# The last block's queries and values by seven half-size products: one more block in a chain, its sums kept in the keys of the block before

## The chip, the cores and the metric

The kernel runs on one core of a Trainium2 chip. Five engines work side by side, each in the order of its own instruction list: TensorE (PE in the profile) multiplies matrices, VectorE (DVE), ScalarE (ACT) and GpSimd (POOL) work on tiles, and SyncE (SP) issues transfers. ACT and POOL issue transfers too. Semaphores order the engines among each other: an instruction waits until a count is reached, and everything behind it on its engine waits with it. The time is the device time of one execution in microseconds (us). The median of three runs stands for the kernel.

## The reference

Two layers work on the same layer-normed input, and a gated sum leaves the kernel:

```python
xn = layernorm(x)                                   # 2 x 2048 rows of 512
q, k, v = norm2(xn) @ qkv                           # a second norm with gamma, beta
s = softmax(causal(q @ k.T / sqrt(512))) @ v @ o_proj + xn
scores = xn @ gate_w.T + gate_b + bias              # 8 experts, the best 2 of each row
y[e] = silu(xn @ w1[e].T + b1[e]) @ w2[e].T + b2[e]  # 512 -> 352 -> 512
g = silu(sum of the 2 chosen experts' y, weighted by a softmax of their scores)
out = x + s * g
```

All of it is in float32.

## The kernel before, in words

The 4096 rows are 32 tiles of 128 rows, in eight blocks of four tiles (`NB = 8`, `TB = 512` rows). The kernel folds the weights first: `wqk` (queries' weight times keys' weight) and `wvo` (values' weight times output weight), each 512 x 512. Then three stages follow, and TensorE runs through all of them.

**Stage 1, projections.** For each block b, `kT` holds the normed rows turned (called keys, 128 partitions x 4 x 512). Two results are made of it: queries `wqk x kT`, stored in `qt_d[b]`, and values `kT x wvo`, stored in `v_d[b]`. An *item* is a pair (block, queries or values): item 0 is the queries of block 0, item 1 its values, and so on. For blocks 0 to 6 (`items`, 14 of them) a 512-cube product is cut into quarters and done by seven half-size products in place of eight, by Winograd's form: four sums of quarters of the weight (`weight_sums`, made once) and four sums of quarters of the keys (`key_sums`, made per block by POOL) stand as factors, and the products are added up in four PSUM banks a to d. `one_product(i, k)` does product k (1 to 7) of item i: four matmuls of 256 columns, then copies by ACT from the bank into the output tile. Product 5 goes to a bank of its own, is copied out as `p5`, and is added to two quarters of the output by DVE (`with_fifth`, L395 in the profile). `chain_of_products()` gives the order: the products of item i end while those of item i + 1 begin. When a queue of stores (`unstored`) is emptied, in product 3, the finished item before is sent to DRAM; from block 5 on by ACT's queue.

Block 7 is done otherwise: `unit(7, u)`, u = 0 to 7, makes a quarter of its queries (0 to 3) or values (4 to 7) by four matmuls of 512 columns, copies the bank into a tile `j` and stores it from ACT's queue. Two of these units stand inside the end of the chain (`None` in `chain_of_products`), six behind it.

**Where the tiles lie.** The memory called `arena` is that of the experts' second weights `w2`, which are loaded late. Until then its six equal areas hold the weight sums of the queries (area 0) and of the values (area 1), the key sums (areas 2 to 4, by `2 + b % 3`) and one output (5). Expert e of `w2` takes three quarters of an area: experts 0 to 2 lie over areas 0, 1 and half of 2. The outputs of items 10, 12 and 13 are in two tiles of the keys' pool `kp` (`late_outs`, `so` in the profile). When stage 1 ends (`stage_a.close()`), the memory of `kp`, of `wqk`/`wvo` and of the staging tiles is given to two later tiles among others: `keep`, a mask that POOL writes (L1414), and `w1s`, sums of the experts' first weights that DVE writes (L1108). Their first writes wait for the last reader of what lay there.

**Stage 2, routing and experts.** `route()` is a generator that turns the gate scores into lists of rows per expert, on DVE mostly. It stands between the last units of stage 1: each `yield n` lets n steps of the projections pass. It ends in `toki` (which rows go into which slot), from which POOL gathers rows, and in the tables `eidi`, `b1sel`, `share`. DVE builds one-hot matrices in eight groups (`at`, `mine`, `which`), and TensorE adds each up with eight small matmuls (`inv_p`, L744). The experts' steps follow. In step i POOL gathers the rows of slot i + 6 (`xs`), SP's queue turns slot i + 4 (`turn`, L1041, `xhT`), DVE joins the halves of slot i + 1 into `xT` (`join`, L1046), PE makes `ph` of slot i (`up`, L1086), ACT scales it into `h`, POOL splits it into `hu` (L1166), SP's queue turns `hu` (L1170), DVE joins it into `ht` (L1175) for slot i - 2, ACT applies silu, and PE makes `py` of slot i - 3 (`down`, L1195). So steps 0 to 2 have no `down`, and step 3 has the first. The expert of a slot is known only at run time, so `down` reads all of `w2`. The first weights' sums `w1s` are made in steps 0 to 6, by DVE but for one.

**Stage 3** is the attention, with the rest.

The order of every engine's instructions is the program's own (`manual_schedule`); no planner moves them. Loads of `w2` come from SP's queue: three transfers for each expert (512 KB, 192 KB, and 2 KB of `b2`). SP's and ACT's transfers signal on eight semaphores taken in turn, and each transfer waits, on the engine that issues it, for the one that last used its semaphore.

Of the kernel before, what the change touches and what calls it, by code (L numbers as in the profile page):

```python
# [26 lines left out]
def gated_attention_moe(  # L27
# [411 lines left out]
    def unit(b, u):  # L439

        kT = kts[b]
        po = banks[(u + 3) % ND]
        r = u % ND
        for c in range(ND):
            if u < ND:
                nc.tensor.matmul(
                    po, lhsT=wqk[:, c, ts(r, P)], rhs=kT[:, c, :],
                    start=(c == 0), stop=(c == ND - 1),
                )
            else:  # L450
                nc.tensor.matmul(
                    po, lhsT=kT[:, c, ts(r, P)], rhs=wvo[:, c, :],
                    start=(c == 0), stop=(c == ND - 1),
                )
        o = stg.tile([P, TB], F32, name=f"j_{b}_{u}", tag="stg")
        nc.scalar.copy(o, po)
        nc.scalar.dma_start(out=(qt_d if u < ND else v_d)[b][:, r, :], in_=o)

# [19 lines left out]
    def key_sums(b):  # L478

        assert all(k != b for _, _, _, k in pending)  # L480
        s = ksums[b] = four(2 + b % 3)
        b11, b12, b21, b22 = (
            kts[b][:, 2 * i : 2 * i + 2, ts(j, HD)] for i in range(2) for j in range(2)
        )
        nc.gpsimd.tensor_tensor(s[:, 0], b12, b11, ALU.subtract)
        nc.gpsimd.tensor_tensor(s[:, 1], b22, s[:, 0], ALU.subtract)
        nc.gpsimd.tensor_tensor(s[:, 2], b22, b12, ALU.subtract)
        nc.gpsimd.tensor_tensor(s[:, 3], b21, s[:, 1], ALU.subtract)
# [4 lines left out]
    items = [(b, of_q) for b in range(SEVEN) for of_q in (True, False)]  # L493
    FIFTH = {}

    def chain_of_products():
        yield from ((0, k) for k in (1, 5, 2, 6))
        for i in range(len(items) - 1):
            for j, k in (1, 1), (0, 3), (0, 7), (1, 5), (0, 4), (1, 2), (1, 6):
                yield i + j, k  # L500
        for k in (None, 3, 7, None, 4):
            yield len(items) - 1, k

    def one_product(i, k):
# [4 lines left out]
        b11, b12, b21, b22 = (  # L509
            kts[b][:, 2 * i : 2 * i + 2, ts(j, HD)] for i in range(2) for j in range(2)  # L510
        )
        if k == 2 and i in (first_late, first_late + 2):
# [4 lines left out]
            else late_outs[int(i == first_late + 2)] if k in (2, 3, 7, 4) else raw[:, : ND * D]  # L517
# [28 lines left out]
        elif k == 5:  # L546
            multiply(bank_d, s[:, 0], t[:, 0], start=True)
            FIFTH[i] = stg.tile([P, TB], F32, name=f"p5_{i}", tag="stg")
            nc.scalar.copy(FIFTH[i], bank_d)
        elif k == 2:  # L550
            multiply(bank_a, a12, b21)
            nc.scalar.copy(place(0, 0), whole(bank_a))
        elif k == 6:
            multiply(bank_b, s[:, 1], t[:, 1])
# [8 lines left out]
        elif k == 7:  # L563
            multiply(bank_c, s[:, 2], t[:, 2])
            with_fifth(place(1, 1), bank_c)
            del FIFTH[i]
        else:
            multiply(bank_c, a22, t[:, 3])
            nc.scalar.copy(place(1, 0), whole(bank_c))
# [9 lines left out]
    def route():  # L579

        with ExitStack() as rt:
# [210 lines left out]
            for i in range(FIRST):  # L792
                gather(i)

# [21 lines left out]
            nc.vector.tensor_copy(eidi, eid)  # L816
            nc.vector.tensor_scalar(eid, eid, -1.0, float(E), ALU.mult, ALU.add)
# [91 lines left out]

    def pieces():  # L910

        n = 0
        for i, k in chain_of_products():
            if k is None:
                unit(*units.pop(next(j for j, (b, _) in enumerate(units) if b == SEVEN)))
                yield
                continue
# [8 lines left out]
        while units:  # L926
            add_due(0)
            unit(*units.pop(0))
            while unstored:
# [1011 lines left out]
```

## Time and profile before

| | us |
|---|---|
| median of three runs | 1008.28 (1007.41 to 1008.75) |
| the profiled execution | 1007.83 |
| its span (first to last instruction) | 1006.0 |
| PE busy in the span | 999.9 |
| start of item 13's product 1 on PE | 198.51 |
| start of the first unit of block 7 | 212.23 |
| start of the first `up` | 246.92 |
| start of the first `down` | 256.39 |
| start of `keep` on POOL | 247.15 |

The profile says when each instruction began and how long it took. In a row of the timeline the first number is the start, the second the time, then engine, line and tiles; "x8" counts records, and a float32 matmul leaves two. Brackets give the idle time of that engine just before the row, and what ended it. ACTq and SPq are the issuing parts of ACT and SP. "KB each, us to landing" is the median time from a transfer's issue to its completion, where the trace has it. TensorE's granted clock is 1.0 through the whole span.

### The profile page before, as it was taken

The numbers are of one execution on the slowest core, as the hardware profiler recorded it, in microseconds if no ns is written. First come the engines' busy times: TensorE is split into PE (matmuls) and PEld (weight loads), VectorE is DVE, ScalarE is ACT, GpSimd is POOL, SyncE is SP. The second block draws the span as 40 slices with busy tenths as digits, with TensorE's granted clock in tenths as the row PEclk, the third lists the DMA queues.
The fourth block names the chain that finished last, engine by engine and source line by source line (L and its number), as shares of the span: only waits on it lengthen the run. The fifth ranks groups of instructions, "written<-read, shape, count | busy, mean of one in ns | idle before, by whom it ended". The sixth has DMA issues, their size and how long they took to land. (4 is left out here: it accounts for less than half of the span.)

```text
span 1006.0 us, 13431 instructions
## 1 busy us (share of the span) xinstructions
PE 999.9 (99%) x3924; PEld 665.3 (66%) x3924; DVE 716.9 (71%) x1396; ACT 403.2 (40%) x804; POOL 483.3 (48%) x475
## 2 busy tenths in 40 slices
PE   9999999999999999999999999999999999999998
PEld 5888888874567767766753448677675544447577
DVE  6996746897887777677744579668576556878667
ACT  3344445322444454444445112232335535442241
POOL 4474564004644454444332165254557776764272
PEclk9999999999999999999999999999999999999999
DMA  8689996978999999999999576274677768753361
GB/s 293 193 264 293 329 286 258 349 249 240 202 227 220 211 208 221 217 200 222 216 218 242 164 193 147 78 206 104 183 199 239 225 200 240 207 141 86 92 165 42
DMA packets 296647, 207.96 MB, mean 207 GB/s; under 512 B 230776, under 2 KB 243832, under 8 KB 296576
## 3 DMA queue, kind: packets, MB, share of 16 engines
q1 hardware_dynamic: 282432, 163.56, 63.2%
q0 software_dynamic: 10400, 34.63, 12.5%
q10 hardware_dynamic: 3744, 8.91, 2.4%
q8 instruction: 34, 0.56, 0.2%
q14 instruction: 37, 0.30, 0.1%
HBM read 92.35 MB, written 60.03 MB: 151 GB/s over the span
## 5 line engine op out<-in xcount | busy, mean ns | idle before, releaser
L1195 PE MATMUL py<-arena,ht 128*128 (+3 forms) x396 | 176.7, 593 | 0.0
L1307 PE MATMUL ps<-k,q 128*128 128x512 f32 (+3 forms) x416 | 143.0, 495 | 0.3 <-PEq L1455 0.3
L1495 POOL COPY pu<-pT 128x1024 uint16<-128x1024 uint16 (+2 forms) x74 | 82.5, 1146 | 118.1 <-ACT pT L1485 59.1
L1166 POOL COPY hu<-h 128x704 uint16<-128x704 uint16 x66 | 61.9, 956 | 155.8 <-issue 121.7
L1195 PEld LDWEIGHTS py<-arena,ht 128*128 128x128 f32 (+3 forms) x396 | 71.8, 185 | 80.7 <-issue 76.9
L1307 PEld LDWEIGHTS ps<-k,q 128*128 128x128 f32 x416 | 74.7, 190 | 67.1 <-issue 56.5
L970 POOL DMA_INDIRECT xs<-zu_d,toki x66 | 77.6, 1176 | 70.2 <-DVE toki L791 55.6
L1181 ACT ACTIVATE ht<-ht,b1sel 128x128 f32<-128x128 f32 (+3 forms) x216 | 67.9, 380 | 88.1 <-DVE ht L1175 88.1
L1145 DVE TENSOR_TENSOR h<-p,h 128x176 f32<-128x176 f32 x182 | 55.5, 337 | 60.7 <-PE p L1138 57.2
L1678 POOL DMA_INDIRECT yg<-y_d,posi x64 | 67.4, 1053 | 36.9 <-DVE yg L1689 21.9
L1535 PE MATMUL po<-v,pT 128*128 128x512 f32 x152 | 67.9, 592 | 0.0
L347 POOL COPY zu<-z 128x1024 uint16<-128x1024 uint16 x32 | 39.9, 1245 | 55.7 <-DVE z L332 55.7
L1517 DVE COPY pT<-puT 128x1024 uint16<-128x1024 uint16 (+2 forms) x74 | 54.1, 759 | 8.8 <-DMA puT<-pu 8.6
L1485 ACT ACTIVATE pT<-pT,nm 128x1024 f32<-128x1024 f32 x14 | 16.1, 1148 | 110.3 <-DVE nm L1395 72.0
L1203 ACT COPY y<-py 128x512 f32<-128x512 f32 x55 | 32.2, 585 | 62.3 <-PE py L1195 48.4
L1485 ACT ACTIVATE pT<-ps,nm 128x512 f32<-128x512 f32 (+3 forms) x52 | 30.1, 581 | 62.5 <-DVE nm L1395 38.8
L1365 DVE TENSOR_TENSOR pT<-p,pT 128x512 f32<-128x512 f32 x49 | 32.9, 687 | 25.8 <-PE p L1359 22.1
L1535 PEld LDWEIGHTS po<-v,pT 128*128 128x128 f32 x152 | 28.6, 190 | 31.9 <-issue 30.1
L1707 POOL TENSOR_TENSOR o<-o,yg 128x512 f32<-128x512 f32 x30 | 42.0, 1398 | 14.3 <-DVE o L1699 14.1
L1699 DVE SCALAR_TENSOR_TENSOR o<-xo,xscale,o 128x512 f32<-128x512 f32 x30 | 25.9, 871 | 30.1 <-ACT o L1696 30.1
L1046 DVE COPY xT<-xhT 128x1024 uint16<-128x1024 uint16 x66 | 45.2, 712 | 2.3 <-DMA xhT<-xs 2.0
L1708 POOL TENSOR_TENSOR o<-o,xo 128x512 f32<-128x512 f32 x30 | 43.0, 1432 | 2.4
(342 smaller groups left out, 2142.9 us busy)
## 6 DMA issues: line engine op xcount, KB each, us to landing
y_d<-y SPq DMA_DIRECT2D x66, 256.0 KB, 4.4
zu_d<-zu SPq DMA_DIRECT2D x32, 264.0 KB, 2.8
kt_d<-kT SPq DMA_DIRECT2D x16, 512.0 KB, 5.9
q<-qt_d SPq DMA_DIRECT2D x32, 256.0 KB, 5.4
k<-kt_d SPq DMA_DIRECT2D x32, 256.0 KB, 4.7
v<-v_d SPq DMA_DIRECT2D x32, 256.0 KB, 5.6
xo<-in_x_dram SPq DMA_DIRECT2D x32, 256.0 KB, 3.8
x<-in_x_dram SPq DMA_DIRECT2D x30, 256.0 KB, 4.9
```

What stands on the lines that cost most here:

```text
L970: nc.gpsimd.indirect_dma_start(out=xs, out_offset=None, in_=zu_d, in_offset=bass.IndirectOffsetOnAxis(ap=toki[:, order[i] : order[i] + 1], ...
L1046: nc.vector.tensor_copy(xT.bitcast(U16).rearrange("p c (t h) -> p c t h", h=2), xhs.pop(i).rearrange("p (h c) t -> p c t h", h=2),)
L1145: nc.vector.tensor_tensor(out, x, y, ALU.add)
L1166: nc.gpsimd.tensor_copy(hu[:, :, :H], h.bitcast(U16).rearrange("p (d h) -> p h d", h=2))
L1181: nc.scalar.activation(ht[:hn, c, at], ht[:hn, c, at], AF.Silu, bias=b1sel[:hn, c, j : j + 1])
L1195: nc.tensor.matmul(py[at, :], lhsT=ht[:k, c, at], rhs=rhs[n], start=(c == 0), stop=(c == NH - 1),)
L1307: nc.tensor.matmul(ps[:, :w], lhsT=aqs[seq[s] // 2][:, c, ts(t % 2, P)], rhs=aks[first + j][:, c, :w], start=(c == 0), stop=(c == ND - 1),)
L1485: nc.scalar.activation(turned[s][:, at:end], src, AF.Exp, bias=nm, accum_out=rs[:, j : j + 1])
L1495: nc.gpsimd.tensor_copy(pu[:, : 2 * w].rearrange("p (h d) -> p h d", h=2), turned[s][:, k : k + w].bitcast(U16).rearrange("p (d h) -> p h ...
L1517: nc.vector.tensor_copy(turned[s][:, k : k + w].bitcast(U16).rearrange("p (i t h) -> p i t h", t=P, h=2), puT[:, : 2 * w // P, :].rearrang ...
L1535: nc.tensor.matmul(dst, lhsT=turned[s][:, ts(k, P)], rhs=avs[first + k // BT][:, k % BT, cols], start=(start and k == k0), stop=(k == k1 - 1),
L1678: nc.gpsimd.indirect_dma_start(out=y, out_offset=None, in_=y_d, in_offset=bass.IndirectOffsetOnAxis(ap=posi[k][:, n : n + 1], axis=0),)
```

## The change

Items 14 and 15 (block 7's queries and values) join the chain, so stage 1 has 16 items of seven products. `unit` is gone. What goes with it:

- `key_sums(7)` writes its four sums over the quarters of the keys of block 6, one or two at a time, behind products 1, 2 and 3 of item 13, which are the last to read those quarters. POOL does it, ahead of its first gathers.
- The outputs of items 14 and 15 go to the two `late_outs`, those of items 12 and 13 before. The stores go out from ACT's queue, those of item 15 behind the last product.
- In the last step products 6 and 2 change places, and product 2 of item 15 empties the queue of stores.
- `w2` of expert 3 is loaded fifth; experts 0, 1 and 2, which lie over the weight sums, are loaded behind the last product in SP's order, behind the first four turns of `xs` and ahead of the fifth.
- `route()` has two more `yield 1`.
- In steps 0 to 4 `join` is done two slots ahead; DVE thus does slots 0 to 2 ahead of its first `w1s`.

```diff
-    def unit(b, u):
-        kT = kts[b]
-        po = banks[(u + 3) % ND]
...
     def key_sums(b, parts=range(4)):
-        s = ksums[b] = four(2 + b % 3)
+        s = ksums[b] = (
+            [four(2 + b % 3)[:, k] for k in range(4)] if b < SEVEN
+            else [quarter_keys(b - 1)[k] for k in (1, 0, 2, 3)]
+        )
+        b11, b12, b21, b22 = quarter_keys(b)
+        of = (b12, b11), (b22, s[0]), (b22, b12), (b21, s[1])
+        for k in parts:
+            nc.gpsimd.tensor_tensor(s[k], *of[k], ALU.subtract)
-    items = [(b, of_q) for b in range(SEVEN) for of_q in (True, False)]
+    items = [(b, of_q) for b in range(NB) for of_q in (True, False)]
     def chain_of_products():
         yield from ((0, k) for k in (1, 5, 2, 6))
         for i in range(len(items) - 1):
-            for j, k in (1, 1), (0, 3), (0, 7), (1, 5), (0, 4), (1, 2), (1, 6):
+            last = i == len(items) - 2
+            for j, k in (1, 1), (0, 3), (0, 7), (1, 5), (0, 4), *(((1, 6), (1, 2)) if last else ((1, 2), (1, 6))):
                 yield i + j, k
-        for k in (None, 3, 7, None, 4):
+        for k in 7, 3, 4:
             yield len(items) - 1, k
...
-            else late_outs[int(i == first_late + 2)] if k in (2, 3, 7, 4) else raw[:, : ND * D]
+            else late_outs[int(i in (first_late + 2, first_late + 4))] if k in (2, 3, 7, 4) else raw[:, : ND * D]
...
         elif k == 2:
             multiply(bank_a, a12, b21)
             nc.scalar.copy(place(0, 0), whole(bank_a))
+            while unstored and i == len(items) - 1:
+                store(*unstored.pop(0))
...
             for i in range(FIRST):
                 gather(i)
+            yield 1
...
             nc.vector.tensor_copy(eidi, eid)
+            yield 1
...
+    SUMS_BEHIND = {1: (0, 1), 2: (2,), 3: (3,)}
...
             one_product(i, k)
+            if i == 2 * SEVEN - 1 and k in SUMS_BEHIND:
+                key_sums(SEVEN, SUMS_BEHIND[k])
             scale_next()
             n += 1
             if n * 4 // 7 > (n - 1) * 4 // 7:
                 units.pop(0)
+                if not units:
+                    add_due(0)
+                    while unstored:
+                        store(*unstored.pop(0))
                 yield
...
-    w2_left = [4, 5, 6, 7, 0, 1, 2, 3]
+    w2_left, w2_last = [4, 5, 6, 7, 3], [0, 1, 2]
...
-            if done >= W2_FROM:
+            if done >= W2_FROM and w2_left:
                 load_w2(w2_left.pop(0))
...
-        if i + 1 not in xts:
-            at(join, 1)
+        for k in (1, 2) if 0 <= i < 5 else (1,):
+            if i + k not in xts:
+                at(join, k)
...
             next(projected)
-            if w2_left:
-                load_w2(w2_left.pop(0))
-    while w2_left:
-        load_w2(w2_left.pop(0))
+    for e in w2_left + w2_last:
+        load_w2(e)
     stage_a.close()
```

More of the change, by code (lines that the diff above doesn't have):

```diff
@@ L437, in keep_scores @@
         )
-    def unit(b, u):
-        kT = kts[b]
-        po = banks[(u + 3) % ND]
[L443 to L457, printed above, removed]
     SEVEN = NB - 1
@@ L476, in weight_sums, with quarter_keys, key_sums @@
         lhs_sums(wsums[name], w)
[L478 removed]
+    def quarter_keys(b):
+        return [kts[b][:, 2 * i : 2 * i + 2, ts(j, HD)] for i in range(2) for j in range(2)]
+    def key_sums(b, parts=range(4)):
         assert all(k != b for _, _, _, k in pending)
[L481 to L493 removed]
+        s = ksums[b] = (
+            [four(2 + b % 3)[:, k] for k in range(4)] if b < SEVEN
+            else [quarter_keys(b - 1)[k] for k in (1, 0, 2, 3)]
+        )
+        b11, b12, b21, b22 = quarter_keys(b)
[3 more added lines that the diff above has]
+    items = [(b, of_q) for b in range(NB) for of_q in (True, False)]
     FIFTH = {}
@@ L508, in one_product @@
         a11, a12, a21, a22 = (w[:, 2 * j : 2 * j + 2, ts(i, HD)] for i in range(2) for j in range(2))
-        b11, b12, b21, b22 = (
-            kts[b][:, 2 * i : 2 * i + 2, ts(j, HD)] for i in range(2) for j in range(2)
-        )
+        b11, b12, b21, b22 = quarter_keys(b)
         if k == 2 and i in (first_late, first_late + 2):
@@ L546, in one_product @@
         elif k == 5:
-            multiply(bank_d, s[:, 0], t[:, 0], start=True)
+            multiply(bank_d, s[:, 0], t[0], start=True)
             FIFTH[i] = stg.tile([P, TB], F32, name=f"p5_{i}", tag="stg")
@@ L552, in one_product @@
             nc.scalar.copy(place(0, 0), whole(bank_a))
+            while unstored and i == len(items) - 1:
+                store(*unstored.pop(0))
         elif k == 6:
-            multiply(bank_b, s[:, 1], t[:, 1])
+            multiply(bank_b, s[:, 1], t[1])
             nc.scalar.copy(bank_c, bank_b)
@@ L563, in one_product @@
         elif k == 7:
-            multiply(bank_c, s[:, 2], t[:, 2])
+            multiply(bank_c, s[:, 2], t[2])
             with_fifth(place(1, 1), bank_c)
+        else:
+            multiply(bank_c, a22, t[3])
+            nc.scalar.copy(place(1, 0), whole(bank_c))
             del FIFTH[i]
-        else:
-            multiply(bank_c, a22, t[:, 3])
-            nc.scalar.copy(place(1, 0), whole(bank_c))
             queue = nc.sync if b < LATE else nc.scalar
@@ L913, in pieces @@
         for i, k in chain_of_products():
[L914 to L917, printed above, removed]
             made[0] = n
@@ L924, in pieces @@
                 units.pop(0)
+                if not units:
+                    add_due(0)
+                    while unstored:
+                        store(*unstored.pop(0))
                 yield
[L926 to L929, printed above, removed]
-                store(*unstored.pop(0))
-            yield
     def sum_keys(i):
```

## The prediction

> **What bounds the kernel now.** I read the page's shares first, then the waits of PE, then the timeline of each engine from 185 to 275 us, where stage 1 ends. The chain that ended last goes back only to 568 us and does not reach the change.
>
> ```profile
> PE 999.9 (99%) x3924; PEld 665.3 (66%) x3924; DVE 716.9 (71%) x1396; ACT 403.2 (40%) x804; POOL 483.3 (48%) x475
> ...
> PE warm L870 <- DVE b1s L181: 1.1, 1, 1.1
> ```
>
> PE is busy 999.9 of 1006.0 us and its longest wait anywhere is 1.1 us, at the start. So PE work that goes away is time, one for one, unless PE has to wait instead; and there is no idle time of PE to pay with. PE's timeline around the change:
>
> ```profile
> 210.50 1.89 PE L526 MATMUL bank_b<-arena 128*128 128x256 f32 x8
> ...
> 223.60 1.11 PE L744 MATMUL inv_p<-which,at 128*128 128x136 bf16 x16
> ...
> 226.32 3.60 PE L446 MATMUL bank_b<-kT,wqk 128*128 128x512 f32 x8
> 229.76 3.60 PE L446 MATMUL bank_c<-kT,wqk 128*128 128x512 f32 x8
> ...
> 246.92 9.63 PE L1086 MATMUL ph<-w,xT 128*128 x32
> 256.39 2.74 PE L1195 MATMUL py<-arena,ht 128*128 x6
> ```
>
> From start to start a unit takes 3.435 us (226.32 to 229.76) and a half-size product 1.727 (210.50 to 212.23, the first unit). The four `up` fill 246.92 to 256.4, and the first `down` follows with no gap. What it waited for is in the rows of DVE, ACT, POOL and SP's queue, in this order:
>
> ```profile
> 222.85 0.72 DVE L777 TENSOR_TENSOR which<-mine,tile 128x544 bf16<-128x544 bf16 x1
> ...
> 247.12 0.89 DVE L1108 TENSOR_TENSOR w1s<-w 128x704 f32<-128x704 f32 x1 [6.23 <-PE bank_c L451]
> ...
> 254.96 0.59 DVE L1175 COPY ht<-huT 128x768 uint16<-128x768 uint16 x1 [2.64 <-DMA huT<-hu]
> ...
> 230.95 9.05 ACTq L575 DMA_DIRECT2D v_d<-so  x2
> ...
> 240.05 0.59 ACT L456 COPY j<-bank_c 128x512 f32<-128x512 f32 x1 [9.51 <-DVE so L395]
> ...
> 247.15 0.20 POOL L1414 MEMSET keep<- 128x128 f32 x1 [6.00 <-PE bank_c L451]
> ...
> 250.16 0.81 POOL L1166 COPY hu<-h 128x704 uint16<-128x704 uint16 x1 [0.38 <-ACT h L1164]
> ...
> 229.93 11.76 SPq L1041 DMA_TRANSPOSE xhT<-xs  x5
> ```
>
> Three things are to be seen. `keep` on POOL and the first `w1s` on DVE stood idle 6 us and began when PE ended its last unit, whose memory they take. From `keep` a chain leads to the first `down`: `keep`, a gather, `hu` at 250.16, its turn from 251.00 landing for `ht` at 254.96, silu from 255.59, `down` at 256.39. That chain had at most 0.4 us to spare. And a store that waits stops ACT: the two `v_d<-so` held ACT's queue 9 us, and the copy of a bank behind them came 9.5 us late (PE wrote that bank again only at 243.49, so it cost nothing).
>
> **The change, part by part.**
>
> *PE work.* Eight units go, 8 x 3.435 = 27.5 us; fourteen products come, 14 x 1.727 = 24.2. Sum: -3.3 us.
>
> *Key sums of block 7.* Four POOL operations of 1.27 to 1.49 us (the rows of the earlier key sums). POOL is idle from 170 to 225.8 us, and nine products or more (15 us) lie between product 1 of item 13 and the first use. Nothing; without that cover up to 5.5 us.
>
> *ACT copies.* Eight of 0.59 us go and fourteen come; ACT is busy 5.0 of 22 us there. Nothing in themselves.
>
> *DVE's adds and the index groups.* Item 13's two adds (1.29 us) now stand ahead of the last group, which ended at 223.57 in the trace (222.85 + 0.72). Group seven ends at 219.75, so the adds run to 220.97 and the last group takes 3.2 more: 224.15. PE's order there, from 212.23: products 14/1 and 13/3, eight index matmuls (0.47), 13/7, 0.47, 14/5, 13/4, 0.47: it is at the last group at 222.27. **PE waits 1.9 us.** `toki`, and with it the gathers from 225.8 and the turns from 229.9, stay where they were within 0.2 us; PE's last twelve products follow from 224.67 on, 1.727 each.
>
> *Stores on ACT.* The two `v_d` stores of item 13 stand ahead of the copy that frees bank c for product 14/4; the second waits for the semaphore of the first turn (`xhT`, 229.93; turns land after 3.9 to 7.6 us, median 5.8). With 5.1 it is 235.0, the copy ends 236.05, and 14/4, due at 235.03, begins at 236.2: **1.1 us** (0 to 2.5).
>
> *Second weights behind.* The program's waits say more than the diff here. Expert 0's first transfer (512 KB) stands in SP's queue behind the fourth turn, so it is issued at about 240.0 (the fourth turn ended at 239.65 in the trace, the fifth began at 240.28). The store of item 14's queries on ACT waits for the same semaphore, so for that load to land; behind the store stand the copies of item 15, one of which frees bank c for the last product, 15/4. How long does the load take? Two bounds:
>
> ```profile
> qt_d<-so ACTq DMA_DIRECT2D x4, 512.0 KB, 6.3
> ...
> v_d<-so ACTq DMA_DIRECT2D x2, 512.0 KB, 3.1
> v_d<-j ACTq DMA_DIRECT2D x4, 256.0 KB, 4.7
> ```
>
> From below 3.1, from above 8.4 (the slowest `so` store). The Trainium skill, "DMA: Bandwidth & Descriptors", section "Anatomy of one DMA", gives 2.0 us and the bytes at 436 GB/s, here 3.2 us (fitted on GpSimd's path). I take 6.0: the load is on the queue of two turns still under way, and a turn in this stretch took up to 7.6; the DMA engines are busy 0.93 from 225 to 247. So it lands at 246.0, the two stores are issued by 246.7, the copy of bank c ends at 247.35, and 15/4, due at 244.85, runs from 247.5 to 249.2: **2.6 us**. By the rule it would land at 243.2 and cost nothing here.
>
> *The last stores.* Item 15's two stores follow the copy of 15/4: issued 249.95 to 250.65. They read `late_outs`, which lie in the memory of `keep` and `w1s`, and both now wait for these stores to land, where they waited for PE before. While they fly, so do item 14's stores and expert 2's load. If stores of ACT's queue ran beside SP's loads undisturbed, 3.1 would do. The same page, section "Issuing engines are not separate DMA queues", speaks against this change: transfers issued from different engines run on the same 16 engines and interleave. With that, 4.7: between the median of all `so` stores (4.3) and the 6.3. So `keep` begins at **255.0**, not 247.15; with 3.1 at 253.4.
>
> *Where it goes next.* Queued behind `keep` on POOL are the seventh gather and `hu` of slot 0; behind `w1s` on DVE the join of slot 3. `hu` follows `keep` after 2.8 us, takes 0.8, its turn lands 3.0 to 4.0 later, join and first silu take 1.0: `down` 8.4 us behind `keep` (9.2 in the trace, with what it had to spare, and the quicker turns that follow, 2.8 us). So `down` begins at 263.4 against 256.39: **+7.0 us**. Slot 3's join is done at 255.0 + 1.8 + 0.7 = 257.5; its `up`, due at 256.3, waits 1.2 of that. The early joins help slots 1 and 2 alone, which were never late. From `down` on the order is the old one, and PE full: the shift stays to the end.
>
> *Sum.* -3.3 + 1.9 + 1.1 + 2.6 + 4.7 (PE free at 258.7, `down` at 263.4) = +7.0. The profiled execution would be 1007.83 + 7.0 = 1014.8 (span 1013.0), the median 1008.28 + 7.0 = **1015.3**. By the two rules' short durations alone (3.2 for load and stores) `keep` begins at 251.3, `down` at 259.7: +3.3, 1011.6.
>
> **Rivals.**
>
> *The saving comes through (faster).* It is PE's pace that sets the end. Place: `keep`'s wait. For -2.0 us `down` must begin by 254.4, so `keep` by 246.0. For it: POOL and DVE were idle there, and the DMA engines' row of this stretch falls to one tenth at 246. Against it: with the index wait the last product ends at 245.4 at the earliest, its copy and two issues take 1.3, the quickest such store 2.6: 249.3. Without any wait it would be -3.3, 1005.0; with the index wait alone -1.4, no longer faster by what can be told.
>
> *The waits on PE are real, the gate has cover.* If `hu` and its turn had more to spare than I read, what is left is -3.3 + 1.9 + 1.1 + 2.6 = +2.3: 1010.6. For it: the four `up` give PE 9.5 us of work after the last product. Against: the gate falls 6 us behind the last product, and the chain from it takes 8.4.
>
> *Crowded DMA.* The load lands at 248 and the stores take 6.5: `keep` at 259, `down` at 267.4, +11: 1019.3. For it: both durations were seen within this stretch. Beyond, more than 1020.
>
> *Quick DMA.* Load by 243 and stores in 3: `keep` at 251, or near 249.5 with no wait on PE but the index one: +1.5 to +3, the upper part slower, the lower no change.
>
> **How the numbers follow.** A measurement of this kernel tells apart what differs by 0.2%, 2.0 us. The likeliest case, the gate of the last stores with its load between 3.2 and 8 us, spans 1011.6 to 1019.3 and has 0.68; crowded beyond 1019.3: 0.10; the gate covered: 0.10; quick DMA with no change: 0.08; the saving through: 0.04. So slower 0.88, same 0.08, faster 0.04. The range 1010.3 to 1020.0 leaves out the two last cases and the far end of crowding.
>
> **What would show it.** Products of items 14 and 15 at 1.73 us each; 1.5 to 2 us of PE's idle ahead of the last eight index matmuls, put down to DVE `which`; ACT held at the `qt_d<-so` stores until after 243; `keep` and `w1s` waiting for a transfer of `v_d`, and starting after 250; a gap of PE ahead of the first `down`. I am wrong if `keep` begins before 249, if the first load lands within 3 us, or if `down` follows `up` with no gap although `keep` is late.

## The result and the profile after

The changed kernel takes 1026.49 us (median of 6 runs, 1024.28 to 1028.56), the kernel before 1008.41 (6 runs beside it): 1.0183 times as long, 95% interval 1.0169 to 1.0197, that is +18.1 us where +7.0 was predicted. The profiled execution has a span of 1024.4 us against 1006.0. One run of e10 below, 1043.41 us, was in a slower state of the chip; its figures are of the other three.

The page's shares and, under the dots, the waits of PE in the changed kernel (line waited for, us in total, times, longest):

```profile
PE 1000.9 (98%) x3972; PEld 676.0 (66%) x3972; DVE 724.7 (71%) x1400; ACT 405.9 (40%) x810; POOL 486.8 (48%) x479
...
PE ph L1067 <- DVE xT L1027: 6.8, 1, 6.8
PE inv_p L725 <- DVE which L758: 4.4, 3, 2.9
PE bank_c L505 <- ACT so L518: 2.8, 2, 1.5
PE py L1176 <- ACT ht L1162: 1.8, 1, 1.8
...
PE p L1119 <- issue: 1.1, 1, 1.1
```

Where PE's longest wait had been 1.1 us, at the start, there are now five kinds of wait, 16.9 us together, all between 200 and 295 us. PE's timeline there (start, us, engine, line, operation, idle time before it and its end):

```profile
213.16 1.89 PE L505 MATMUL bank_a<-kT,wqk 128*128 128x256 f32 x8
214.89 1.89 PE L505 MATMUL bank_b<-arena,kT 128*128 128x256 f32 x8
...
227.37 0.63 PE L725 MATMUL inv_p<-which,at 128*128 128x136 bf16 x8 [2.92 <-DVE which L758]
...
250.08 2.00 PE L505 MATMUL bank_c<-wvo,kT 128*128 128x256 f32 x8 [1.27 <-ACT so L518]
251.93 7.34 PE L1067 MATMUL ph<-w,xT 128*128 x24
266.07 4.88 PE L1067 MATMUL ph<-w,xT 128*128 x8 [6.80 <-DVE xT L1027]
272.75 2.85 PE L1176 MATMUL py<-arena,ht 128*128 x6 [1.80 <-ACT ht L1162]
```

The products stand 1.73 us apart, as costed. The first `up` starts at 251.93 (246.92 before), the first `down` at 272.75 (256.39): +16.4 us. The fourth `up` took 4.88 us where the three ahead of it took 7.34 together. The rows of the other engines behind these waits:

```profile
200.83 2.29 DVE L747 TENSOR_TENSOR at<-lane,part 128x1024 bf16<-128x1024 bf16 x1
...
212.48 1.80 DVE L752 TENSOR_TENSOR mine<-slot_b,part 128x544 bf16<-128x544 bf16 x1
...
217.47 1.67 DVE L758 TENSOR_TENSOR which<-mine,row 128x544 bf16<-128x544 bf16 x1
...
248.50 0.82 ACTq L556 DMA_DIRECT2D qt_d<-so  x2
...
252.73 1.07 ACTq L556 DMA_DIRECT2D v_d<-so  x2
...
263.61 0.20 POOL L1394 MEMSET keep<- 128x128 f32 x1 [20.09 <-DMA v_d<-so]
...
263.60 0.89 DVE L1089 TENSOR_TENSOR w1s<-w 128x704 f32<-128x704 f32 x1 [11.04 <-DMA v_d<-so]
```

Three rows of DVE are each about 1 us longer than their like (`at` is 1.22 elsewhere, `mine` and `which` 0.72). The last two stores are issued from 252.73 on, and `keep` and `w1s` wait for them until 263.6.

The third view is one that the prediction did not use: busy time of the engines in long stretches, of before and then of after (from:to, length, PE, PEld, DVE, ACT, POOL, granted clock, mean share of the DMA engines, GB/s).

```profile
212.00:232.00 20.00, 20.00 (x88) 12.13 (x87) 18.29 (x32) 5.60 (x9) 4.95 (x5) 1.00 0.75 248
232.00:248.00 16.00, 16.00 (x40) 7.31 (x39) 9.47 (x15) 2.93 (x5) 4.44 (x12) 1.00 0.99 289
```

```profile
212.00:232.00 20.00, 16.27 (x99) 14.08 (x98) 18.97 (x25) 4.68 (x9) 5.90 (x4) 1.00 0.28 96
232.00:248.00 16.00, 14.48 (x68) 12.47 (x66) 11.56 (x23) 5.64 (x10) 5.12 (x13) 1.00 0.98 263
248.00:264.00 16.00, 10.00 (x36) 6.31 (x34) 2.90 (x5) 4.05 (x6) 0.32 (x2) 0.99 0.91 244
```

From 212 to 232 us the kernel before moves 20 x 0.248 = 5.0 MB, the changed one 1.9 MB. By queue (packets, MB, share of the engines; q1 is SP's queue, q10 ACT's), before and then after:

```profile
q1 hardware_dynamic: 1443, 2.69, 40.6%
q10 hardware_dynamic: 576, 1.57, 21.5%
```

```profile
q10 hardware_dynamic: 288, 1.05, 14.5%
q1 hardware_dynamic: 386, 0.72, 10.7%
```

So 2.0 of the 3.0 MB belong to SP's queue: they are the second weights of experts 0 to 2, which now wait behind the last product. Half a MB belongs to ACT's stores and another half to POOL's gathers, which begin 3.3 us later. The outputs leave otherwise too. A unit's output was complete, and stored in a piece of 256 KB, every 3.4 us. An item of seven products has its four quarters complete only near its end, and the outputs of the last three items leave after 235 us in pieces of 512 KB. Loads and stores thus come later, into the stretch in which the turns fill the DMA engines already. The number of bytes alone does not make that stretch dear: from 232 to 264 us the changed kernel moves 8.1 MB and the kernel before 7.4.

### The profile page after: what moved, and what is told of

It is laid out like the page before. It is cut to its first block, busy times and chain, and to the rows that moved or that the text cites. A ratio compares the mean times of both kernels' runs of the same rounds, so it can differ in the third digit from the quotient of the medians.

```text
span 1024.4 us, 13531 instructions
## 1 busy us (share of the span) xinstructions
PE 1000.9 (98%) x3972; PEld 676.0 (66%) x3972; DVE 724.7 (71%) x1400; ACT 405.9 (40%) x810; POOL 486.8 (48%) x479
## 5 line engine op out<-in xcount | busy, mean ns | idle before, releaser
L951 POOL DMA_INDIRECT xs<-zu_d,toki x66 | 76.4, 1157 | 25.2 <-issue 11.4
L1687 POOL TENSOR_TENSOR o<-o,yg 128x512 f32<-128x512 f32 x30 | 41.7, 1389 | 14.3 <-DVE o L1679 14.2
L1067 PE MATMUL ph<-w,xT 128*128 (+1 forms) x112 | 37.7, 485 | 6.8 <-DVE xT L1027 6.8
```

The costliest lines, as they stand in the source:

```text
L951: nc.gpsimd.indirect_dma_start(out=xs, out_offset=None, in_=zu_d, in_offset=bass.IndirectOffsetOnAxis(ap=toki[:, order[i] : order[i] + 1], ...
```

## The experiments

Each kernel ran beside the kernel before, whose median was 1008.0 to 1008.5 each time. Medians in us, ratio to before with its interval:

| Run | Changed kernel, but | Median | Ratio | Interval |
|---|---|---|---|---|
| (none) | as it is | 1026.49 | 1.0183 | 1.0169-1.0197 |
| e1 | item 15's output in its own memory | 1023.29 | 1.0155 | 1.0139-1.0172 |
| e4 | without the late second weights | 1022.85 | 1.0138 | 1.0111-1.0165 |
| e5 | PE kept busy ahead of the fourth `up` | 1025.72 | 1.0177 | 1.0152-1.0201 |
| e6 | without block 7's key sums | 1022.76 | 1.0144 | 1.0104-1.0184 |
| e10 | late weights issued by POOL | 1023.00 | 1.0152 | 1.0130-1.0173 |
| e12 | `keep` and `w1s` later | 1026.80 | 1.0182 | 1.0148-1.0216 |
| e13 | e10 and e12, index groups mended | 1020.32 | 1.0125 | 1.0104-1.0145 |
| e15 | item 12's output stored early, six times, in place of items 13 to 15 | 1014.66 | 1.0059 | 1.0042-1.0076 |
| e16 | e12 and e1, index groups mended, last stores on SP | 1020.57 | 1.0157 | 1.0094-1.0220 |
| e17 | e15, index groups mended | 1009.00 | 1.0009 | 0.9999-1.0019 |
| e18 | e17, joins one slot ahead | 1007.58 | 0.9999 | 0.9988-1.0009 |
| e19 | joins one slot ahead | 1025.78 | 1.0158 | 1.0137-1.0180 |

Two runs add one part of the change to the kernel before: e2 the key sums (1010.98, 1.0030, 1.0019 to 1.0041), e3 the late second weights (1014.60, 1.0065, 1.0048 to 1.0082).

Two cautions hold for all that follows. Single repairs that give back about 3 us (e1, e6, e10) have intervals that touch or overlap the changed kernel's, so their worth is known only roughly. And the executions differ before the change begins: item 13's product 1 starts at 198.51 in the trace of before, at 198.61 in the changed kernel's, and up to 199.96 in the others. Differences of places below 1.4 us between two traces are therefore not read as effects of an edit.

### One part of the change alone

**e2: four sums as in the change, used by nothing, added to the kernel before.**

```diff
+            if i == 2 * SEVEN - 1:
+                unused_sums(k)
...
+        for n in {1: (0, 1), 2: (2,), 3: (3,)}.get(k, ()):
+            nc.gpsimd.tensor_tensor(s[n], *of[n], ALU.subtract)
```

> The kernel before, with one part of the change alone: POOL makes the four key sums of block 7 over block 6's keys at the same places, and nobody reads them. Theory (POOL's sums hold up DVE's index work): each sum lengthens the DVE row that it meets by about 1 us (2.29 in place of 1.22, 1.80 and 1.67 in place of 0.72), DVE's last index group ends 3 to 4 us later, PE waits 1 to 3 us for groups, 1009.5 to 1012 us. Rival (the sums are free because POOL was idle, as the prediction had it, and the longer DVE rows come from something else): DVE rows keep 1.23 and 0.72, 1008.4 within 0.7.

They cost 2.9 us, as the theory had it: PE waits 1.8 us for index groups where it waited for none. A row of DVE and the row of POOL in the same moment (the trace has rows of three of the four sums):

```profile
201.94 2.29 DVE L766 TENSOR_TENSOR at<-lane,part 128x1024 bf16<-128x1024 bf16 x1
...
201.81 1.34 POOL L916 TENSOR_TENSOR kT<-kT,kT 128x512 f32<-128x512 f32 x1 [29.60 <-PE bank_a L526]
```

The sum starts 0.13 us ahead of `at` and ends 1.21 us after `at` begins; `at` takes 1.07 us longer than its 1.22. The same holds for two rows of `mine` (1.79 each) beside the sums at 212.79 and 220.26. The Trainium skill, "SBUF — State Buffer", section "Who interferes with whom", has the rule: an instruction of DVE with two inputs in SBUF contends with one of GpSimd that reads SBUF, for a port pair that is an exclusive lock. The rows agree: each row of DVE grows by 1.07 us, about the 1.21 us that were left of the sum. So POOL's idle time was no cover; the cover would have had to be DVE's, and DVE is busy without a gap from 195 to 227 us.

**e3: second weights of experts 0 to 2 loaded behind, in the kernel before.**

```diff
-    w2_left = [4, 5, 6, 7, 0, 1, 2, 3]
+    w2_left, w2_last = [4, 5, 6, 7, 3], [0, 1, 2]
...
-    while w2_left:
-        load_w2(w2_left.pop(0))
+    for e in w2_left + w2_last:
+        load_w2(e)
```

> The kernel before, with one part of the change alone: second weights of expert 3 loaded fifth, those of experts 0 to 2 behind the last unit in SP's order, behind four turns. Theory (the late loads hurt only through the stores that stand behind them in a chain, which the units' staging tiles do not form): `keep` still starts when PE ends, loads land before the first `down`, 1008 to 1010.5 us. Rival (late loads by themselves make the first `down` or PE's banks wait): PE idle of 3 us or more ahead of `up` or `down`, 1012 or more.

It costs 6.5 us. ACT's timeline:

```profile
250.26 0.58 ACT L456 COPY j<-bank_d 128x512 f32<-128x512 f32 x1 [9.17 <-DMA arena<-in_b_dram]
...
254.21 0.58 ACT L456 COPY j<-bank_a 128x512 f32<-128x512 f32 x1 [3.37 <-DMA arena<-in_w_t_dram]
```

ACT's stores share semaphores with the loads on SP's queue and wait for them to land; the copies behind them come late, the first `h` at 257.35 (249.54 before), the first `down` at 264.45. This is the prediction's step "second weights behind", and it is dear even where the last block is still made by units: the rival's case. The places are those of the slowest of four executions (1017.64), in which three turns took 10 to 12 us, against 4 to 8 in the trace of before, although they were issued ahead of the first late load. So part of the lateness in this trace is not the loads'.

### One cause at a time taken out of the changed kernel

**e1: item 15's output in a tile of its own** (`stg` gives up two buffers for it).

```diff
-    stg = right(stage_a, name="stg", bufs=4)
+    stg = right(stage_a, name="stg", bufs=2)
...
+            last_out[0] if i == 2 * NB - 1 and k in (2, 3, 7, 4)
+            else raw[:, ts(i % NRAW, ND * D)] if i < first_late
```

> The changed kernel with one thing undone: item 15's output goes to a tile of its own that lies under no later `keep` or `w1s` (the staging pool has 2 buffers in place of 4 to make room). Theory (the last stores gate the experts' start): `keep` and `w1s` no longer wait for the v_d stores, but for the qt_d stores of item 14, issued near 248.5 us, or for PE; `keep` starts near 255 in place of 263.6, PE's idle ahead of the fourth `up` falls from 7 us to under 2, the granted clock stays at 1.0, and 8 to 11 us come back: 1015 to 1019 us. Rival (PE has to wait there anyway, for turns or second weights that are late): less than 3 us come back, 1023.5 or more.

```profile
255.91 0.20 POOL L1398 MEMSET keep<- 128x128 f32 x1 [10.51 <-DMA qt_d<-so]
...
253.71 9.71 PE L1071 MATMUL ph<-w,xT 128*128 x32
265.09 2.85 PE L1180 MATMUL py<-arena,ht 128*128 x6 [1.67 <-ACT ht L1166]
```

`keep` comes at 255.91 and not 263.61, the four `up` run through, and the first `down` is 7.7 us sooner. The profiled execution is 7.0 us shorter, but the medians differ by 3.2: it was the quickest of its four. `keep` came where the theory put it, the time between the two ranges. The memory of the last stores is a gate, as predicted; behind it stand item 14's stores.

**e12: the gate taken away altogether.** `make_keep` holds the memset and the select of `keep`, which stood ahead of the loop over slots.

```diff
-        for _ in range((2, 2, 1, 4, 3, 3, 1)[i] if 0 <= i < paired.start else 0):
+        for _ in range((0, 0, 0, 4, 4, 4, 4)[i] if 0 <= i < paired.start else 0):
...
+        if i == 4:
+            make_keep()
```

> Changed kernel in which nothing near the first down takes the memory of the late outputs: keep is made after slot 4 and the sums of first weights on DVE begin with slot 3, and neither stands ahead of the work for the first down. Theory (the memory of keep and w1s is the gate, and PE's idle time behind it drops the clock): PE's wait for xT ahead of the fourth up goes (6.8 us), the clock stays near 1.0, first down about 262 to 264 and not 272.8, and the time falls by 8 to 11 us, to 1015.5 to 1018.5. Rival (the turns of xT and hu land late of themselves in the crowded stretch): the wait for xT or ht stays over 4 us, first down behind 267, and the time not below 1021.

```profile
256.55 3.78 PE L505 MATMUL bank_c<-wvo,kT 128*128 128x256 f32 x8 [6.44 <-ACT so L518]
...
270.62 2.74 PE L1176 MATMUL py<-arena,ht 128*128 x6
```

The gate is gone and nothing is won. The rival's time and first `down` are right, but the wait stands in a third place. Here the first late load, issued at 246.75, landed only by 254.9, and ACT's `qt_d` stores, issued at 254.98, waited for it, so PE waited 6.4 us for bank c instead of 6.8 for `xT`. That load took 8.2 us here and 3.8 in the changed kernel, but also 6.3 in e19, whose program is the changed kernel's up to there. So the trace shows one way in which the time is lost without the gate; that nothing is won, the medians show.

**e4: without the late loads** (the outputs of experts 0 to 2 are then wrong).

```diff
-    for e in w2_left + w2_last:
+    for e in w2_left:
```

> The changed kernel without the loads of the second weights of experts 0, 1 and 2, so what these experts give is left wrong; all else stays, but the semaphores shift by nine transfers. Theory (the 2.1 MB of second weights crowd the last stores, and hold ACT through the shared semaphores): the v_d stores are issued 1 to 2 us earlier and land in 4 to 6 us in place of 9 to 10, `keep` starts near 256, 1016 to 1020 us. Rival (the stores are slow because item 14's stores are ahead of them on ACT's queue and turns are under way): they still take 8 us or more, 1022.5 or more.

```profile
238.56 1.07 ACTq L556 DMA_DIRECT2D v_d<-so  x2
...
251.64 0.59 ACT L531 COPY so<-bank_a 128x512 f32<-128x512 f32 x1 [6.17 <-DMA v_d<-so]
```

3.6 us come back, a time between the two ranges. The last stores now land in 2.6 and 3.6 us, as the theory had it, but `keep` starts at 262.69: item 13's two stores, issued from 238.56 beside the turns, took 13.0 and 14.2 us with no late load in flight (5.5 and 5.9 in the trace of the changed kernel), and a copy into the same memory waited for them.

**e10: the late loads issued by POOL**, so that ACT's stores share no semaphore with them.

```diff
-        load_w2(e)
+        load_w2(e, nc.gpsimd)
```

> Changed kernel with the second weights of experts 0 to 2 issued by POOL and not by SP, so that ACT's stores no longer share a semaphore with them; the bytes are the same and are issued earlier (from about 236 us, each as PE is done with its memory). Theory (ACT is held by the shared semaphore): ACT issues item 15's stores about 2.5 to 3 us sooner, PE's second wait for bank c goes, keep begins some 3 us sooner if a store then takes the same 10 us, and the time falls by 2.5 to 4 us, to 1022.5 to 1024. Rival (what counts is how slowly transfers land in this stretch, whoever holds whom): stores take as much longer as they are issued sooner, and the time stays within 1.5 us of 1026.5.

3.5 us come back, within the theory's range: the second wait for bank c is gone, and the last stores are issued at 251.38. But they took 6.9 and 8.9 us, `keep` began at 261.07, 9.7 us behind the first issue (10.9 in the changed kernel), and PE waited 5.7 us for `xT`; in that the rival was right. The loads were expected from 236 us on; POOL issued them from 249.91.

**e5: 32 useless matmuls ahead of the fourth `up`.**

```diff
+        if i == 3:
+            busy = ps_a.tile([P, TB], F32, name="busy", tag="a")
+            for _ in range(32):
+                nc.tensor.matmul(busy[:, :P], lhsT=ident, rhs=ident, start=True, stop=True)
```

> Changed kernel with 32 matmuls of 128x128 of no use put on PE ahead of the fourth up, in the place where PE stood idle 6.8 us and the granted clock then read 0.50. Theory (the fourth up took 4.88 us and not 2.5 only for the clock): the clock in the rows from 264 to 272 us stays near 1.0, the fourth up takes about 2.5 us, and the time falls by 2 to 2.5 us against the changed kernel, to about 1024. Rival (the slow up is a wait for its joins or for weights in disguise, or the clock does not follow PE's own work): the fourth up stays near 4.9 us and the time within 1 us of 1026.5.

```profile
261.25 7.31 PE L1063 MATMUL busy<-ident 128*128 128x128 f32 x64
268.40 2.53 PE L1071 MATMUL ph<-w,xT 128*128 x8
```

The granted clock stays at 1.00 from 256 to 272 us (0.50 from 264 to 270 in the changed kernel), and the fourth `up` takes 2.53 us and not 4.88. So the slow `up` was the clock, as the theory had it (the useless work itself, 64 in the row for the 32 calls, ran until 268.4). Yet the time is not distinct from that of the changed kernel, because the fourth `up` was not what the first `down` waited for: from `keep` to the first `down` it is 9.17 us here, 9.15 in the changed kernel with its half clock, and 9.18 in e1, where the clock read 1.00. It waited for `ht`, made from the turn of slot 0's `hu`. In the changed kernel:

```profile
268.31 3.48 DVE L1089 TENSOR_TENSOR w1s<-w 128x704 f32<-128x704 f32 x1
...
271.71 0.55 DVE L1156 COPY ht<-huT 128x768 uint16<-128x768 uint16 x1
...
268.66 1.67 POOL L1089 TENSOR_TENSOR w1s<-w 128x704 f32<-128x704 f32 x1
```

The turn had landed by 270.2. `ht` stood behind a sum of first weights that takes 0.88 us elsewhere and took 3.48 beside POOL's sum and the copy behind it: the same meeting of DVE and POOL as in e2, about 1.5 us. Here DVE's row began first, and was still the one that grew.

**e6: without the four sums** (block 7's queries and values are then wrong).

```diff
-                key_sums(SEVEN, SUMS_BEHIND[k])
+                key_sums(SEVEN, ())
```

> Changed kernel with the four key sums of block 7 left out (its queries and values are then made from what lies there, so they are wrong; the products and their number stay). Theory (POOL's sums lengthen the DVE rows they meet by about 1 us each): PE's waits for DVE's which in the index groups fall from 4.4 to about 1.9 us, all of it in the last group, ahead of which item 13's adds stand; first up about 3 us sooner, and the time about 3 us below the changed kernel, 1023 to 1024. Rival (the adds and the moved order make the wait, the sums nothing): the waits stay at 4 us or more, and the time within 1 us of 1026.5.

```profile
PE ph L1067 <- DVE xT L1027: 5.0, 1, 5.0
PE bank_c L505 <- ACT so L518: 3.7, 1, 3.7
PE py L1176 <- ACT ht L1162: 2.2, 1, 2.2
PE inv_p L725 <- DVE which L758: 1.6, 1, 1.6
```

The index wait falls from 4.4 to 1.6 us, which is what the adds alone make, and the predicted 1.9 was right for them. 3.7 us come back, in four runs from 1020.3 to 1028.0, so wide that the interval overlaps the changed kernel's. The other waits stay, and the first `up` is no sooner in this trace (252.06): the wait for bank c, 3.7 us, stands ahead of it.

### The transfers

Each of these moved or shortened one wait, and another of 4 to 7 us stood elsewhere. That pointed to what they all wait for.

**e15: the same bytes stored early.** The six stores of items 13 to 15 carry item 12's output and are issued as soon as that is complete.

```diff
-            unstored.extend(((qt_d if of_q else v_d)[b], g, outs[:, g], queue) for g in range(2))
+            if i < 2 * SEVEN - 1:
+                unstored.extend(((qt_d if of_q else v_d)[b], g, outs[:, g], queue) for g in range(2))
+            if i == 2 * SEVEN - 2:
+                for dst in v_d[SEVEN - 1], qt_d[SEVEN], v_d[SEVEN]:
+                    unstored.extend((dst, g, outs[:, g], nc.sync) for g in range(2))
```

> Changed kernel in which the six stores of items 13 to 15 are issued early: they take item 12's output as soon as that is complete, on SP's queue ahead of the late second weights, and the outputs of items 13 to 15 themselves are not stored (block 6's values and block 7's queries and values are wrong). All products, copies, adds, loads and the number of bytes stay; 3 MB of stores leave the stretch of the turns for the one from 212 to 232 us, in which the DMA engines of the changed kernel stood nearly idle. Theory (stores of whole items, which come ready in lumps at the end, meet the turns and the late loads on the same DMA engines, and every wait behind bank c follows from it): the four turns take 6 to 7 us and not 10, the late loads land within 4 us, no wait for bank c, keep and w1s follow PE's last product by 1 to 2 us, no idle time ahead of the fourth up, the clock stays near 1.0, and what is left is -3.3 and the index wait of 5.0: 1009.5 to 1012. Rival (late loads and turns are enough to crowd the stretch, without the stores): the turns still take 9 us or more, idle time ahead of the fourth up or the first down stays over 3 us, and the time is 1016 or more.

```profile
212.00:232.00 20.00, 16.28 (x91) 13.88 (x90) 18.62 (x28) 4.07 (x7) 4.99 (x3) 0.92 0.85 300
```

```profile
251.64 9.63 PE L1071 MATMUL ph<-w,xT 128*128 x32
261.59 2.85 PE L1180 MATMUL py<-arena,ht 128*128 x6 [0.33 <-ACT ht L1166]
...
252.48 0.29 POOL L1398 MEMSET keep<- 128x128 f32 x1 [7.43 <-ACT so L549]
```

11.8 us come back. The waits for bank c and `xT` are gone, `keep` follows the last copy, and the four `up` run through: the theory's case in the main. The turns landed 5.7 to 7.6 us after their issue (4.1 to 8.5 in the changed kernel), so they gained little. The time is 2.7 us above the theory's range because the index wait of 2.92 us was followed here by a clock of 0.62 (228 to 232 us), in which one product took 3.3 us instead of 1.78, and by 1.9 us of small waits behind the first `down`.

The edit does three things at once: it takes 3 MB of stores out of the stretch of the turns, it takes the last stores out of ACT's queue, where they stood behind the late loads, and it leaves `keep` and `w1s` no store to wait for. e12 does the third alone and wins nothing, e10 the second and wins 3.5 us; e13 below does both, with the index groups mended and the stores in their place, and stays 11.3 us above e17. That points to the place of the stores, but e13 lets slot 0's `hu` stand behind the loads on POOL, so the three are not fully told apart.

**e17: e15 with the index groups mended.** The second sum is made by DVE, the third and fourth by DVE behind the groups; item 13's adds come behind them too.

```diff
+    SUMS_BEHIND = {
+        (2 * SEVEN - 1, 1): [((0,), nc.gpsimd), ((1,), nc.vector)],
+        (2 * SEVEN + 1, 1): [((2, 3), nc.vector)],
+    }
...
-            deferred.append((made[0], nc.vector.tensor_tensor, (out, out, whole(FIFTH[i]), ALU.add)))
+            deferred.append((made[0] + (4 if i == 2 * SEVEN - 1 else 0), nc.vector.tensor_tensor, (out, out, whole(FIFTH[i]), ALU.add)))
```

> The kernel of early stores (items 13 to 15 not stored, item 12's output stored early in their place, so block 6's values and block 7's queries and values are wrong) with the index groups mended besides: the second sum of block 7's keys on DVE in its place, the third and fourth on DVE behind the index groups, item 13's adds behind them. Theory (stores in lumps and index wait are the two causes, and what is left is the work saved): index waits below 1 us, first up at about 246.0 to 247.0, first down within 10.5 us of it, and 1005.5 to 1009. Rival (with PE sooner, the late loads and turns become the next wait): a new wait of over 2 us ahead of the first down, and 1010 or more.

```profile
224.01 0.63 PE L729 MATMUL inv_p<-which,at 128*128 128x136 bf16 x8 [0.67 <-DVE which L762]
...
245.26 9.63 PE L1074 MATMUL ph<-w,xT 128*128 x32
255.79 2.85 PE L1183 MATMUL py<-arena,ht 128*128 x6 [0.90 <-ACT ht L1169]
```

1009.0 us: with the stores moved and the index groups mended, 17.5 of the 18.1 us are back, at the edge of the theory's range. The first `up` is 1.7 us sooner than in the kernel before, the first `down` 0.6, in an execution that ran 0.4 us late when the change began. This is no kernel to use: the outputs of items 13 to 15 are not stored.

**e13 and e16: what can be mended with all stores in place.** e13 has e17's index groups with e10's loads and e12's `keep`. e16 has the loads on SP again, e1's tile, and item 15's stores on SP:

```diff
-            queue = nc.sync if b < LATE else nc.scalar
+            queue = nc.sync if b < LATE or i == 2 * NB - 1 else nc.scalar
```

> Changed kernel with four things mended at once: the first sum of block 7's keys on POOL as before, the second on DVE in its place and the other two on DVE behind the index groups; item 13's adds behind the index groups; the late second weights issued by POOL; keep after slot 4 and the sums of first weights on DVE from slot 3. Theory (waits of index groups, ACT and the memory gate add up, and each part mended comes back): index waits below 1 us, bank c waits below 1 us, no wait for xT, and 1006 to 1013. Rival (the turns, the stores and the late loads fill the DMA engines from about 232 to 258 us whatever waits for them): the index waits go, but a wait of 4 us or more stays somewhere ahead of the first down, and the time is 1016 to 1022.

> A kernel with all stores and all loads in which everything found is mended as far as memory allows: index groups as in the run before it; item 15's output in a tile of its own and its two stores on SP's queue, ahead of the late second weights, so that none of ACT's stores waits for those; keep after slot 4, sums of first weights on DVE from slot 3. Theory (stores and late loads still share the DMA engines with the turns, and the first down now waits for the late weights or for its own turn behind them): no wait above 1 us ahead of the first up (at 246 to 247.5), a wait of 2 to 6 us ahead of the first down, and 1010 to 1016. Rival (the order of issue was what cost, and the bytes find room): first down at 257 or before, and 1006 to 1009.

In e16:

```profile
245.90 9.71 PE L1074 MATMUL ph<-w,xT 128*128 x32
264.94 4.61 PE L1183 MATMUL py<-arena,ht 128*128 x6 [9.34 <-ACT ht L1169]
```

PE goes into the first `up` at 246.83 (e13) and 245.90 (e16), as good as before the change or better, and then waits 7.8 and 9.3 us ahead of the first `down`: slot 0's `hu` and its turn stand behind the late loads, in POOL's queue in e13 and in SP's in e16. The medians are 1020.3 and 1020.6: of e13 the rival's case, of e16 dearer than both of its expectations (its ratio is drawn up by one run of four, 1032.4). With every byte stored, no order tried here gets below +12 us.

**e18 and e19: joins one slot ahead as before the change**, in e17 and in the changed kernel.

```diff
-        for k in (1, 2) if 0 <= i < 5 else (1,):
+        for k in (1,):
```

> The kernel of early stores with the index groups mended (items 13 to 15 not stored, item 12's output in their place), with joins one slot ahead as before the change. Theory (joins two ahead put two copies of DVE ahead of the sums of first weights and so make the wait of 1.2 us for xs behind the seventh up): that wait goes, and the time falls to 1007 to 1008.3. Rival (that wait comes from POOL's copies of h being slowed by DVE's sums, whatever the order of joins): the wait stays and the time stays within 0.8 us of 1009.0.

> Changed kernel with joins one slot ahead as before the change. Theory (two ahead only helps slots 1 and 2, which are not late; with w1s late, DVE's queue stands either way): first down within 1 us of 272.8 and the time within 1.5 us of 1026.5. Rival (the early joins kept the second and third up going while DVE waited, and so were needed): PE waits for xT ahead of the second or third up, first down is 2 us or more later, and the time 1028.5 or more.

In e17 and e15 PE waits 1.2 us for `xs` behind the seventh `up`; in e18 that wait is gone and the median is 1.4 us lower, as the theory had it (the intervals overlap). Its profiled execution was one of the two longest of 13 (1011.9), with a wait of 3.0 us ahead of the first `down`; its first three turns took 8.7 to 9.5 us although no store stood beside them. In e19 PE waits for `xT` ahead of the third `up` (3.3 us), and the first `down` is 2.0 us later, which was the rival's sign. From there to the end of the span it takes 749.8 us, as in the kernel before (749.6) and not as in the changed one (751.7). The time is the theory's: the same within what four runs tell. So the early joins win 2.0 us ahead of the first `down` and lose 1.8 behind it; what they are worth on the whole these runs can't tell from nothing.

## Why the prediction was right or wrong

The direction and the chain were right, and none of the signs that the prediction named for being wrong came. The size was not right: 11.4 us are missing in the sum of the profiled execution (1013.0 predicted as its span, 1024.4 measured). Step by step, from the timelines above:

| Point | Predicted | Measured | Added to the error |
|---|---|---|---|
| First product behind the index groups | 224.67 | 227.84 | +3.2 |
| First `up` | 249.2 | 251.93 | -0.4 |
| Last stores issued from | 249.95 | 252.73 | 0.0 |
| `keep`, `w1s` | 255.0 | 263.6 | +5.8 |
| First `down` | 263.4 | 272.75 | +0.8 |
| End of the span | 1013.0 | 1024.4 | +2.0 |

- *PE work, -3.3*: right in the pace of the products. In e17 1.7 of it stands at the first `up`, behind an index wait of 0.9, and none in the total.
- *Key sums, "nothing"*: **the first step that failed.** The cover named was POOL's idle time. e2 puts 2.9 us on them, because they stop DVE's index rows, and e6 takes 2.8 us out of the index wait without them. The bound given for the case without cover (5.5) held it; the value taken did not.
- *Adds and index groups, 1.9*: right for the adds (1.6 in e6).
- *Stores on ACT, 1.1, and second weights behind, 2.6*: the mechanism, ACT held by a semaphore that it shares with SP's loads, was right (e3, e10). The sizes came out by luck: 1.5 and 1.3 us were measured. The first load took 3.8 us, near the 3.2 that the prediction set aside and not its 6.0, but was issued at 244.64, 4.6 us later than reckoned; the two errors cancelled in part.
- *The last stores, 4.7 us*: **the second step that failed, and the largest.** From the first issue to `keep` it was 10.9 us and not 5.05; the two stores took 9.3 and 10.0 us to land. The sum took a duration between two medians of the kernel before (4.3 and 6.3) as if it belonged to the store, and put the slowest one, 8.4, only at the edge. The 3.1 us that it calls undisturbed is a single store (issued 239.68) that flew beside two turns with the DMA engines full (0.99 from 232 to 248 us), so it measures no quiet either. It should have asked what else is in flight and when: the outputs of three items in lumps, the late loads and the turns. It had quoted the section that says so, and allowed 1.6 us for it. e15 gives back 11.8 us, for the gate, the waits for bank c and the clock behind the gap together.
- *`down` 8.4 behind `keep`*: 9.15. The sum left out DVE's `w1s` beside POOL's, which held `ht` by about 1.5 us (the rows at e5); the half clock of the fourth `up` cost nothing here.
- *"From `down` on the order is the old one"*: **a third step that failed, by 2.0 us.** The change itself puts the joins two ahead, and e19, with one ahead, takes 1.8 of them back behind the first `down` (and loses 2.0 ahead of it).

Of the rivals, crowded DMA came nearest, and its far end, "beyond, more than 1020", had 0.10. e12 shows that the gate, on which the likeliest case rested, was not needed for the loss: without it PE stopped at bank c.

Left open is why these transfers land so late. It is not the stores' company alone. The changed kernel, e5, e12 and e19 are the same program up to there (but for one gather in e12), and no late load was in flight yet when these stores were issued; still item 13's two stores took 5.5 and 5.9, 5.5 and 6.2, 8.0 and 10.9, and 8.3 and 10.8 us. Turns go the same way: 4 to 8 us in some traces, 9 to 15 in others (e3, e4, e10, e12, e13, e16, e19), and 9 in e18, without those stores. In e4, from 246 to 252 us, the DMA engines show a share above 1 at 79 to 104 GB/s: much time and few bytes. What puts an execution into the one kind or the other no run here shows, and traces of different kinds, those of e12 and of the changed kernel among them, are compared with that doubt. It does not touch the medians.

## What to carry to other kernels

Before a change that replaces outputs spread over time by outputs that come ready together, add up the bytes that each stretch moves before and after it, for each queue: here the loads that had to wait for their memory were more of it than the outputs. Transfers that lose their place in a quiet stretch come back where the DMA engines are full, and then every wait that can be named is only the next one in line. The bytes tell where the trouble will be, not its size; a transfer's duration there can differ by a factor of two from one execution to the next. Idle time of one engine covers work only if no neighbour has to stand still for it. Where several single repairs each give little and the wait moves, look for what all the waits have in common, and test it in one run that moves as few other things as it can.

## What the runs showed of the hardware

- **A sum on POOL stops DVE.** Fp32 subtractions of 1.3 to 2.0 us on POOL lengthened single bf16 rows of DVE by 0.95 to 1.08 us (three in the changed kernel, three in e2), and a row of `w1s` took 3.48 us instead of 0.88 beside POOL's 1.67 and the copy behind it.
- **The clock follows idle time.** After 6.8 us without work PE's granted clock read 0.50 for 6 us and 4.88 us were needed for 2.5 us of work. After 2.9 us, at the same index wait, it read 0.57 to 0.66 from 228 to 232 us in seven traces (e1, e4, e5, e10, e12, e15, e19) and 1.00 in that of the changed kernel. The Trainium skill, "TensorE: Matmul & The Clock Gate", section "What's actually happening", gives half rate after an idle window of about 3.4 us; the first case agrees, and the seven traces show that 2.9 us can be enough.
- **Transfers beside turns land after very different times.** Stores of 512 KB took 3.1 and 5.4 us in this stretch of the kernel before, 5.5 and 5.9 in the changed kernel, 8.3 and 10.8 in e19 with the same program up to there, and 13.0 and 14.2 in e4. The changed kernel's last two, with late loads and a turn under way, took 9.3 and 10.0. The cause stays open.
